# Query order, fill places and mask matmuls in a fused block-sparse, gated LoRA kernel on one Trainium2 core

## The chip, the cores and the metric

The kernel runs on one core of one Trainium2 chip. A core has a matrix engine (TensorE, in the profile PE, with its weight loads as PEld), a vector engine (VectorE, DVE), a scalar engine (ScalarE, ACT), a general engine (GpSimd, POOL) and a queue engine (SyncE, SP). Every engine works through its own list of instructions in order and waits at semaphores for the others. Transfers between the chip's memory and the core's on-chip buffers (DMAs) are issued by SP, ACT and POOL and run beside the engines. Matrix products land in PSUM, a small accumulator memory of which a buffer here holds 128 x 512 values.

The metric is the device time of one execution in microseconds (us). Three runs of the kernel before gave 449.41, 449.87 and 450.09 us; their median, 449.87, is the time before.

## What is computed

The input x is (2, 1024, 1024): two batches of 1024 rows. Cut to what matters:

```python
xn = layernorm(x)                                   # over the last axis, eps 1e-5
bm = (mask summed over each 32 x 32 block) > 0
s  = xn @ (weight * bm spread to blocks).T + bias   # S
q  = xn.mean(over the 1024 rows) @ Wq.T             # one query per batch
c  = softmax(q @ lora_keys.T / sqrt(128))           # 8 coefficients per batch
y  = xn @ W_org.T + sum_e c[e] * (xn @ lora_down[e]) @ lora_up[e]
out = x + s * silu(y)
```

All weights are 1024 x 1024, `lora_down` is 8 x 1024 x 64 and `lora_up` 8 x 64 x 1024.

## The kernel before, in words

**Precision and folding.** A value in float32 is split into a high part that the matrix engine takes (type fp32r) and the remainder; a product is the sum of high x high, high x low and low x high, so that one logical matmul is three on TensorE (lines 453, 456, 457 for S and Y tiles, 417 to 419 for folds, 1216 for the last stage). The low-rank part is not run on x. Instead its weights are folded into W_org, once per batch, since the coefficients differ by batch: a *fold* takes one 128 x 512 piece of W_org transposed and adds the product of `lora_down` with the scaled `lora_up` to it. `y_prep` (L401) loads `ds` and `wo` over the SP queue and splits `ds` into `dhi` (ScalarE, L408) and `dlo` (VectorE, L409); `y_mul` (L412) runs twelve matmuls into a buffer `psw`; `y_sum` (L422, L424) adds `psw` to `wo` on VectorE. `scale_up` (L387) loads four pieces of `lora_up`, scales each by its coefficient on ScalarE (L395) and takes the remainder on VectorE (L396): the four `cut` tiles.

**Stages.** (1) Up to about 90 us a start-up that is ordered by hand: layer-norm statistics of batch 0, its transposes, the first half of S, and the first half of the folded weights for batch 0. (2) `phase("y", 0, 0, ..., jobs_b)`: eight row tiles of Y, 24 matmuls each, and behind each tile one fold of the second half (`mix_jobs`), with statistics of batch 1, the mask of the second half, and the first sums of the transposed batch 1 in `jobs_b`. (3) `phase("y", 0, 1, ..., jobs_c)`: eight more row tiles. Meanwhile `s_mul` (L298) loads a piece of the S weight (`ws`), multiplies it by the block mask `m_sb` (L302) and casts it; `s_lo` (L308, L310) takes the remainder. The query of batch 1 is made here too: `steps[0]` transposes row sums into `xrow` (L325), `steps[1]`, which is `query` (L338), multiplies `xrow` by Wq on VectorE with a running sum (L349) and adds the halves to `qb` (L353). `steps[2]`, `scores` (L358), is set in the middle of row tile 6 by `split_at`: TensorE multiplies `qb` by the keys (L360). (4) Eight row tiles of S (`s_tile`), and between the first five of them the sixteen folds of batch 1, shared out as 4, 4, 3, 3, 2. (5) The last stage computes batch 1 transposed, in eight *units* with seven block products per quadrant in place of eight; the sums of x it needs (`xv`) were stored to memory in stages 2 and 3.

**Fills and unit products.** In stage 4 the sums of x come back: `fill` loads a 128 x 512 piece of `xv` into one of three slots of the buffer `misc` in turn, casts it on ScalarE (L1065) and takes the remainder on VectorE (L1066). The loads of `scale_up(1, 1)`, which the eighth fold issues (`if n == NKT - 1`), use the next three slots of `misc` in the same turn and one buffer of the staging pool. `early` holds the first unit's work on its weights: two mask products (`unit_mask`, L1094) and four block sums (`unit_sum`, L1102). The first five row tiles and their folds are the loop at the end of the change below. `ds`, `wo`, `ws` and `us` share six staging buffers (tag "st"). A `wo` buffer is free when its folded result has been stored to memory (`yu`, issued by ScalarE's queue one fold later, L513).

**The mask.** `mask_part` (L283) loads 128 x 1024 mask values, sums them by rows on ScalarE (L254), and, with the second half of a pair, makes a small tile `r` on VectorE (L264, `mask_spread`), multiplies it by an expansion matrix that lies in `misc[:, 0, :]` (eight matmuls into `mp`, L274, `mask_apply_mm`) and copies the result to `m_sb` (L281, `mask_apply_cp`). `spread_stats` (L927), which follows one of the parts, transposes the statistics of batch 1 into `row_ps` on TensorE (L930).

**Order.** Program order is the order on TensorE, VectorE and ScalarE in stages 2 to 5. The list of the SP queue is arranged when the program is built, so an edit can move a load past others there. In `jobs_b` and `jobs_c` the argument i is the row tile just multiplied; what they yield is emitted behind that tile.

Of the kernel before, what the change touches and what calls it, by code (L numbers as in the profile page):

```python
# [32 lines left out]
def kernel(  # L33
# [102 lines left out]
    def nat_tile(dt=F32):  # L136
        k = turns[0] % 3
        turns[0] += 1
        v = raw_flat[:, k * D : (k + 1) * D]
        return v if dt == F32 else v.bitcast(dt)  # L140
# [107 lines left out]
    def mask_sum(qr, c, mt, eng, part=0):  # L248

        if qr not in msum:  # L250
            msum[qr] = small.tile([P, 2, 2], F32, name="s2")
        o = msum[qr][:, part, c : c + 1]
        if eng is nc.scalar:
            nc.scalar.activation(mt.bitcast(F32), mt, AF.Copy, accum_out=o)  # L254
        else:
            nc.vector.tensor_reduce(o, mt, AX.X, ALU.add)
# [5 lines left out]
    def mask_spread(qr):  # L262
        r4 = small.tile([P, 2, 4], BF16, name="r4")
        nc.vector.scalar_tensor_tensor(  # L264
            r4, msum[qr][:, 0, :].unsqueeze(2).to_broadcast([P, 2, 4]), 0.0,
            pick4.unsqueeze(1).to_broadcast([P, 2, 4]), ALU.is_gt, ALU.mult,
        )
        spread[qr] = r4

    def mask_apply_mm(qr):  # L270
        r4 = spread[qr]
        mp = ps_s.tile([P, NKT, 8], F32, name="mp", tag="ps_s")
        for kt in range(NKT):
            nc.tensor.matmul(  # L274
                mp[:, kt, :], lhsT=expand[:, kt * P : (kt + 1) * P],
                rhs=r4.rearrange("p a b -> p (a b)"), start=True, stop=True,
            )
        spread[qr] = mp

    def mask_apply_cp(qr):  # L280
        nc.vector.tensor_copy(m_sb[:, :, 8 * qr : 8 * (qr + 1)], spread[qr])  # L281

    def mask_part(qr, c, mt=None):  # L283
        if mt is None:
            mt = nat_tile(I32)
        else:
            mt = stage_l.tile([P, D], I32, name="mt", tag="ac", bufs=1)
        nc.sync.dma_start(mt, mask[2 * qr + c])
        mask_sum(qr, c, mt, nc.scalar)
        if c == 1:  # L290
            mask_spread(qr)
            mask_apply_mm(qr)
            mask_apply_cp(qr)

    def new_slot():
        return wpool.tile([P, NKT, 2, NH], F32R, name="slot", tag="w")
# [257 lines left out]
    J = lambda f, *a: (lambda: f(*a))  # L554
# [98 lines left out]
    with tc.manual_schedule(engines={mybir.EngineType.PE, mybir.EngineType.DVE, mybir.EngineType.Activation, mybir.EngineType.Pool}):  # L653
# [237 lines left out]
        def jobs_b(i):  # L891
            if i == 0:
                yield J(scale_up, 0, 1)
            yield J(mix_jobs, y01, 0, 1, i)
            yield J(store_out, 1)
            if i < 3:
                yield J(act_stats, 1 + i)
            for t in ((4,), (5, 6), (7,), (), (), (), (), ())[i]:
                yield J(nat_stats, t)
            yield from {  # L900
                2: [J(mask_part, 2, 0)], 3: [J(mask_part, 2, 1), J(spread_stats), J(mask_part, 3, 0, 1)],
                4: [J(mask_part, 3, 1, 1)],
            }.get(i, ())
            if i == 3:
                yield J(wide_load, 0, 0)
            if i == 4:
                yield J(wide_load, 0, 1)
                yield J(wide_a, 0)
            if i == 5:
                yield J(wide_b, 0)  # L910
                yield J(wide_load, 1, 0)
            if i == 6:
                yield J(wide_a, 1)
            if i == 7:
                yield J(wide_load, 1, 1)
# [63 lines left out]
        def wide_b(j):  # L979
# [12 lines left out]
            store_sums()  # L992

        phase("y", 0, 0, y00, True, jobs_b)


        s1 = new_slot()
        steps = coeffs(1)

        def jobs_c(i):  # L1000
            if i < 2:
                yield J(store_out, 1 - i)

            if i < 6:
                yield J(s_mul, s1, 1, i)
            if i == 5:
                yield steps[0]
                yield steps[1]
            if i == 6:
                yield steps[3]  # L1010
                yield J(scale_up, 1, 0, up_homes)
            if i == 5:
                yield J(s_mul, s1, 1, 6)
                yield J(s_mul, s1, 1, 7)
                for kt in (5, 6, 7):
                    yield J(s_lo, s1, 1, kt)
            if i in (0, 2):
                yield J(wide_load, 2 + i // 2, 0)
                yield J(wide_load, 2 + i // 2, 1)
            if i < 5:  # L1020
                yield J((wide_b, wide_a)[i % 2], 1 + (i + 1) // 2)
                yield J(s_lo, s1, 1, i)

        up_homes = [misc[:, 0, :]]
        split_at[(0, 1, 6)] = steps[2]
        phase("y", 0, 1, y01, False, jobs_c)


        folds = [(h, kt) for h in range(2) for kt in range(NKT)]

        def fold(n):
            h, kt = folds[n]
            if n + 1 < len(folds):
                y_prep(1, *folds[n + 1])
            store_late()
            y_mul(1, h, kt)
            flush()
            y_sum(1, h, kt)
            ps, ws = staged.pop((1, h, kt))
            late_stores.append((  # L1040
                yu[:, :, 2 * h + kt // 4, kt % 4, :].rearrange("u p n -> p u n"),
                ws.rearrange("p (u n) -> p u n", n=P),
            ))
            if n == NKT - 1:
                homes = [misc[:, (len(spare) + k) % 3, :] for k in range(3)]
                spare.extend(homes)
                scale_up(1, 1, homes)
# [23 lines left out]
        def s_tile(i):  # L1071
            store_out()
            flush()
            ps = gemm(0, i, s1)
            pending.append(J(final_evac, "s", 0, 1, i, ps))
# [6 lines left out]
        def unit_load(u, i):  # L1082
            kind, p = units[u]
            src = wu[p] if kind == "s" else yu[p].rearrange("p a j n -> p (a j n)")
            c = slice(2 * i * NH, 2 * (i + 1) * NH)
            nc.sync.dma_start(raw_flat[:, c], src[:, c])
# [45 lines left out]
        def fills(j, n):  # L1132
            for _ in range(n):
                fill(j, ORDER_X[filled[j]])
                filled[j] += 1

        for i, n in enumerate((4, 4, 3, 3, 2)):
            s_tile(i)
            for k in range(n):
                fold(done)  # L1140
                done += 1
                if i < 3 and (i == 2 or k in (1, 2)):
                    fills(0, 1)
                if i > 2 and (i == 4 or k):
                    fills(1, 1)
                if i in (2, 3):
                    early.pop(0)()
            if i == 0:
                unit_load(0, 0)
                unit_load(0, 1)  # L1150
# [219 lines left out]
```

## Time and profile before

| what | value |
|---|---|
| time, median of three runs | 449.87 us (449.41 to 450.09) |
| the profiled execution's own time | 450.43 us |
| its span, first to last instruction | 448.7 us |
| VectorE busy | 288.9 us |
| ScalarE busy | 175.3 us |
| moved to and from memory | 90.58 MB, 202 GB/s over the span |
| TensorE clock granted | full speed in all 40 slices |

The span is what the engines' records cover; the time also holds what lies before and after it. A timeline row reads: start in us, duration, engine, line, operation, output<-inputs, shape, and in brackets the idle time of that engine before the row with what ended it. Matmuls overlap, so a row's duration is longer than the distance to the next start. In the waits view a row names who waited for whom: total us, number of times, longest. SPq and ACTq rows are issues of transfers; a transfer lands some us after its issue (stores of `yu` 2.6 to 7.9 us, median 5.2).

### The profile page before, as it was taken

How to read it: one execution, taken by the hardware profiler on the slowest of the kernel's cores; microseconds unless marked ns; L12 is line 12 of the kernel's file. 1: busy time of each engine (PE TensorE's matmuls, PEld its weight loads, DVE VectorE, ACT ScalarE, POOL GpSimd, SP SyncE). 2: the span in 40 equal slices, each digit the busy share in tenths (PEclk: the TensorE clock that was granted, in tenths of full speed). 3: DMA queues.
4: the chain of work that ended last, by engine and by line, in shares of the span. 5: the costliest groups of instructions: out<-in, count | busy, mean ns of one | idle time of the engine just before them, and what ended most of it. 6: DMA issues, size and time to landing. Idle time of an engine off the chain costs nothing.

```text
span 448.7 us, 5791 instructions
## 1 busy us (share of the span) xinstructions
PE 437.7 (98%) x2058; PEld 363.1 (81%) x2058; DVE 288.9 (64%) x478; ACT 175.3 (39%) x291; POOL 76.5 (17%) x93
## 2 busy tenths in 40 slices
PE   7999999999999999989999999999999999999996
PEld 5789888888878888878888788887888888888885
DVE  5989777756627768855456586578466295455625
ACT  3676626454631222224233234176354422441520
POOL 3784310002320313120000000110020020002000
PEclk9999999999999999999999999999999999999999
DMA  8995406687896799895979898966174247219103
GB/s 266 390 351 203 151 25 200 220 256 192 281 294 196 249 265 314 284 368 166 242 226 314 236 289 260 259 166 210 48 159 145 72 106 177 93 16 220 47 1 117
DMA packets 47741, 90.58 MB, mean 202 GB/s; under 512 B 4816, under 2 KB 15328, under 8 KB 47712
## 3 DMA queue, kind: packets, MB, share of 16 engines
q1 hardware_dynamic: 30624, 66.08, 44.6%
q0 software_dynamic: 6624, 16.26, 15.7%
q10 hardware_dynamic: 10464, 7.87, 5.3%
q8 instruction: 16, 0.26, 0.2%
q14 instruction: 13, 0.11, 0.1%
HBM read 70.26 MB, written 19.93 MB: 201 GB/s over the span
## 4 chain that ended last, share of the span: by engine, by line
PE 68%; DVE 12%; DMA 10%; issue 6%; ACT 3%; POOL 1%; SPq 0%; ACTq 0%; DVEq 0%; POOLq 0%
PE acc_ps L1216 24%; PE py L1216 10%; PE acc_ps L457 7%; PE acc_ps L453 7%; PE acc_ps L456 7%; PE psw L419 4%; PE psw L417 4%; PE psw L418 4%; DMA ws<-in_wT_dram 3%; DMA stash<-in_x_dram 2%; DVE st L148 1%; DMA raw<-in_x_dram 1%; DVE slot L594 1%; DMA misc<-in_up_dram 1%; DMA raw<-in_mask_dram 1%
## 5 line engine op out<-in xcount | busy, mean ns | idle before, releaser
L1216 PE MATMUL acc_ps<-xw,ow 128*128 128x512 f32 (+1 forms) x492 | 112.0, 384 | 0.0
L453 PE MATMUL acc_ps<-slot,xgrp 128*128 128x512 f32 (+1 forms) x288 | 106.5, 370 | 0.1
L457 PE MATMUL acc_ps<-slot,xgrp 128*128 128x512 f32 (+1 forms) x288 | 105.6, 367 | 0.7 <-DVE xgrp L606 0.7
L456 PE MATMUL acc_ps<-slot,xgrp 128*128 128x512 f32 (+1 forms) x288 | 105.7, 367 | 0.6 <-DVE slot L594 0.4
L1216 PEld LDWEIGHTS acc_ps<-xw,ow 128*128 128x128 f32 x492 | 90.8, 188 | 18.7 <-ACT acc_ps L1276 0.5
L456 PEld LDWEIGHTS acc_ps<-slot,xgrp 128*128 128x128 f32 x288 | 54.3, 189 | 10.6 <-DVE slot L594 2.1
L457 PEld LDWEIGHTS acc_ps<-slot,xgrp 128*128 128x128 f32 x288 | 54.2, 188 | 10.3 <-DVE xgrp L606 1.1
L453 PEld LDWEIGHTS acc_ps<-slot,xgrp 128*128 128x128 f32 x288 | 54.3, 188 | 9.1 <-DVE stash L469 0.3
L419 PE MATMUL psw<-cut,dlo 128*128 128x512 f32 x128 | 49.9, 390 | 0.8 <-DVE dlo L409 0.8
L418 PE MATMUL psw<-cut,dhi 128*128 128x512 f32 x128 | 49.8, 389 | 0.0
L417 PE MATMUL psw<-cut,dhi 128*128 128x512 f32 x128 | 49.8, 389 | 0.0
L1216 PE MATMUL py<-xw,ow 128*128 128x512 f32 x192 | 46.3, 389 | 0.0
L1216 PEld LDWEIGHTS py<-xw,ow 128*128 128x128 f32 x192 | 36.0, 188 | 7.5
L1109 DVE TENSOR_TENSOR ow<-raw,ow 128x1024 fp32r<-128x1024 f32 (+1 forms) x32 | 34.5, 1087 | 10.2 <-ACT ow L1108 10.2
L408 ACT CAST dhi<-ds 128x512 fp32r<-128x512 f32 x32 | 19.7, 616 | 45.6 <-DMA ds<-in_down_dram 32.5
L505 POOL DMA_DIRECT2D stash<-in_x_dram x16 | 14.4, 899 | 120.7 <-DVE stash L502 120.7
L409 DVE TENSOR_TENSOR dlo<-ds,dhi 128x512 fp32r<-128x512 f32 x32 | 22.0, 688 | 14.8 <-ACT dhi L408 14.8
L424 DVE TENSOR_TENSOR wo<-wo,psw 128x512 f32<-128x512 f32 x32 | 21.9, 685 | 13.0 <-PE psw L419 12.8
L1108 ACT CAST ow<-raw 128x1024 fp32r<-128x1024 f32 (+1 forms) x32 | 29.4, 939 | 2.1 <-DVE wo L424 1.6
L419 PEld LDWEIGHTS psw<-cut,dlo 128*128 128x128 f32 x128 | 24.0, 188 | 6.2 <-DVE dlo L409 1.3
L418 PEld LDWEIGHTS psw<-cut,dhi 128*128 128x128 f32 x128 | 24.0, 188 | 5.0
L417 PEld LDWEIGHTS psw<-cut,dhi 128*128 128x128 f32 x128 | 24.0, 188 | 4.9
(180 smaller groups left out, 468.4 us busy)
## 6 DMA issues: line engine op xcount, KB each, us to landing
ds<-in_down_dram SPq DMA_DIRECT2D x32, 256.0 KB, 3.8
wo<-in_worgT_dram SPq DMA_DIRECT2D x32, 256.0 KB, 4.2
raw<-in_x_dram SPq DMA_DIRECT2D x11, 512.0 KB, 4.8
stash<-in_x_dram POOLq DMA_DIRECT2D x16, 256.0 KB, 5.2
raw<-in_wu_dram SPq DMA_DIRECT2D x8, 512.0 KB, 5.2
yu<-wo ACTq DMA_DIRECT2D x16, 256.0 KB, 5.2
raw<-yu SPq DMA_DIRECT2D x8, 512.0 KB, 3.8
out_dram<-stash ACTq DMA_DIRECT2D x14, 256.0 KB, 3.9
```

What stands on the lines that cost most here:

```text
L408: nc.scalar.copy(dhi, ds)
L409: nc.vector.tensor_tensor(dlo, ds, dhi.bitcast(F32), ALU.subtract)
L417: nc.tensor.matmul(ps, lhsT=dhi[:, c, :], rhs=u[c][:, 0, :], start=c == 0, stop=False)
L418: nc.tensor.matmul(ps, lhsT=dhi[:, c, :], rhs=u[c][:, 1, :], start=False, stop=False)
L419: nc.tensor.matmul(ps, lhsT=dlo[:, c, :], rhs=u[c][:, 0, :], start=False, stop=c == 3)
L424: nc.vector.tensor_tensor(ws, ws, ps, ALU.add)
L453: nc.tensor.matmul(ps, lhsT=xs[:, kt, 0, cols], rhs=w[:, kt, 0, wc], start=kt == 0, stop=False)
L456: nc.tensor.matmul(ps, lhsT=xs[:, kt, 0, cols], rhs=w[:, kt, 1, wc], start=False, stop=False)
L457: nc.tensor.matmul(ps, lhsT=xs[:, kt, 1, cols], rhs=w[:, kt, 0, wc], start=False, stop=kt == NKT - 1)
L1108: nc.scalar.copy(o[:, a:b, 0], raw[:, a:b])
L1109: nc.vector.tensor_tensor(o[:, a:b, 1], raw[:, a:b], o[:, a:b, 0].bitcast(F32), ALU.subtract)
L1216: nc.tensor.matmul(ps, lhsT=o[:, a, wl, j, :], rhs=xw[j][:, m, xl, cols], start=start and j == 0 and k == 0, stop=j == 3 and k == 2, skip_ ...
```

## The change

Three edits. The mask's matmuls and copy (`mask_apply`) are taken out of `mask_part` and called one row tile later, behind that tile's fold; the small tile `r` is still made at once. In row tile 5 of stage 3 the query (`steps[0]` and `steps[1]`) is emitted ahead of the sixth `s_mul`, not behind it. In stage 4 the seven fills of the first x tile go behind folds 1, 2, 3, 4, 5, 9 and 10, where they went behind folds 1, 2, 5, 6, 8, 9 and 10 (counted from 0), and the six early products of the first unit behind folds 8, 11, 12, 13, 14 and 15, where they went behind folds 8 to 13.

```diff
@@ mask_part @@
         if c == 1:
             mask_spread(qr)
-            mask_apply_mm(qr)
-            mask_apply_cp(qr)
+
+    def mask_apply(qr):
+        mask_apply_mm(qr)
+        mask_apply_cp(qr)
@@ jobs_b @@
                 2: [J(mask_part, 2, 0)], 3: [J(mask_part, 2, 1), J(spread_stats), J(mask_part, 3, 0, 1)],
-                4: [J(mask_part, 3, 1, 1)],
+                4: [J(mask_apply, 2), J(mask_part, 3, 1, 1)], 5: [J(mask_apply, 3)],
@@ jobs_c @@
-            if i < 6:
-                yield J(s_mul, s1, 1, i)
             if i == 5:
                 yield steps[0]
                 yield steps[1]
+            if i < 6:
+                yield J(s_mul, s1, 1, i)
             if i == 6:
                 yield steps[3]
                 yield J(scale_up, 1, 0, up_homes)
@@ row tiles and folds of stage 4 @@
             for k in range(n):
                 fold(done)
                 done += 1
-                if i < 3 and (i == 2 or k in (1, 2)):
+                if i < 3 and k in ((1, 2, 3), (0, 1), (1, 2))[i]:
                     fills(0, 1)
                 if i > 2 and (i == 4 or k):
                     fills(1, 1)
-                if i in (2, 3):
+                if (i, k) in ((2, 0), (3, 0), (3, 1), (3, 2), (4, 0), (4, 1)):
                     early.pop(0)()
```

## The prediction

> **What bounds the kernel now.** I read the busy table, then TensorE's own waits, then its timeline from 50 us to the end, and last the timelines of VectorE, ScalarE and the SP queue around each wait.
>
> ```profile
> span 448.7 us, 5791 instructions
> PE 437.7 (98%) x2058; PEld 363.1 (81%) x2058; DVE 288.9 (64%) x478; ACT 175.3 (39%) x291; POOL 76.5 (17%) x93
> ...
> PE sp L360 <- DVE qb L353: 1.4, 1, 1.4
> PE mp L274 <- DVE r L264: 1.2, 2, 0.6
> PE psw L419 <- DVE dlo L409: 0.8, 1, 0.8
> ...
> 62.34 0.40 PE L457 MATMUL acc_ps<-slot,xgrp 128*128 128x512 f32 x1
> 63.03 0.40 PE L456 MATMUL acc_ps<-slot,xgrp 128*128 128x512 f32 x1
> ...
> 123.14 0.39 PE L419 MATMUL psw<-cut,dlo 128*128 128x512 f32 x1
> 124.12 0.34 PE L274 MATMUL mp<-r,misc 128*128 128x8 bf16 x8 [0.59 <-DVE r L264]
> 124.65 0.39 PE L456 MATMUL acc_ps<-slot,xgrp 128*128 128x512 f32 x1
> ...
> 132.40 0.39 PE L419 MATMUL psw<-cut,dlo 128*128 128x512 f32 x1
> 133.17 0.39 PE L456 MATMUL acc_ps<-slot,xgrp 128*128 128x512 f32 x1
> ...
> 193.50 0.39 PE L457 MATMUL acc_ps<-slot,xgrp 128*128 128x512 f32 x1
> 195.31 0.36 PE L360 MATMUL sp<-keys_sb,qb 128*128 128x8 f32 x2 [1.43 <-DVE qb L353]
> 195.84 0.40 PE L456 MATMUL acc_ps<-slot,xgrp 128*128 128x512 f32 x1
> ...
> 247.56 0.39 PE L418 MATMUL psw<-cut,dhi 128*128 128x512 f32 x1
> 248.78 0.50 PE L419 MATMUL psw<-cut,dlo 128*128 128x512 f32 x1 [0.83 <-DVE dlo L409]
> 249.12 0.40 PE L417 MATMUL psw<-cut,dhi 128*128 128x512 f32 x1
> ```
>
> TensorE starts a 128x512 matmul every 0.227 us (the 24 of the tile at 220.12 end at 225.56). From 50 us on this pitch breaks in three places only, the three waits shown (the other 0.6 us of the mp row is at 12 us). So TensorE sets the end, an engine off it counts only where TensorE waits for it, and a wait's price is read from starts, not from the idle column: start to start less the same stretch without the wait.
>
> **The change, part by part.** *Mask matmuls a tile later.* Between 123.14 and 124.65 lie 1.51 us. The second mask's eight matmuls between the same neighbours take 133.17 - 132.40 = 0.77 us. The row_ps transpose in the first stretch I take at 0.11 us (eight L325 transposes fit between 189.88 and 191.21: 1.33 less two pitches, by 8). So the wait costs 1.51 - 0.77 - 0.11 = 0.63 us. It arises because the mask sum waits for its load (ScalarE's sum ends at 123.87) and VectorE's r follows at 123.90. Moved behind the next tile's product, the matmuls find r some 8 us old; the second set moves to about 140.3, and its r (132.4) is as old. What stood behind them, row_ps, waits for the statistics, whose last power starts on GpSimd at 119.65: no wait. What is moved with them: the PSUM copies to m_sb (0.14 us more on VectorE before the work at 142.75, with dlo due only at 146.6), and in the built order the SP queue's load of misc (133.02, it overwrites the expansion weights) goes behind the ws load at 142.29. Its reader is at 201.39; m_sb's first reader is at 162.36. Both covers are over 20 us. Gain 0.63, from the idle column 0.59.
>
> *Query ahead of the sixth S weight.* The VectorE rows:
>
> ```profile
> 189.56 0.68 DVE L310 TENSOR_TENSOR slot<-ws,slot 128x512 fp32r<-128x512 f32 x1
> 192.92 0.69 DVE L302 TENSOR_TENSOR ws<-ws,m_sb 128x512 f32<-128x512 f32 x1 [2.68 <-DMA ws<-in_wT_dram]
> 193.53 0.68 DVE L349 SCALAR_TENSOR_TENSOR junk<-xrow,misc 128x512 f32<-128x512 f32 x1
> 194.87 0.29 DVE L353 TENSOR_TENSOR qb<-qh 128x128 f32<-128x128 f32 x1
> ```
>
> VectorE is idle for 2.68 us before the s_mul at 192.92, which waits for its load, while the query behind it has had its rows since 191.1 (190.10 + 1.03). Ahead of it the query starts when the s_lo ends (190.24), and qb is there after 194.87 + 0.29 - 193.53 = 1.63 us, at 191.9 (with 0.3 to spare for the second row). TensorE, 0.63 us early, asks at 193.73 - 0.63 = 193.1: no wait, 1.2 us of spare. The s_mul still starts when its load lands, so it loses nothing; the softmax comes some 1.5 us earlier, as VectorE does the three s_mul and three s_lo without a break. The price of the wait: 195.84 - 193.50 = 2.34, against 63.03 - 62.34 = 0.69 for the same two matmuls unhindered: 1.65 us (idle column 1.43).
>
> *Fills and unit products over the folds.* Call T the start of the ninth fold (241.88), index 8. The eleventh's L419 is due at T + 5.44 + 0.45 = T + 5.89 and ran at T + 6.90; between its neighbours 249.12 - 247.56 = 1.56 less two pitches leaves 1.11 us lost. Its dlo started at 248.04 = T + 6.16, and TensorE followed 0.74 later. VectorE was held by the third scaled up-tile, then ran without a break:
>
> ```profile
> 236.35 0.46 SPq L392 DMA_DIRECT2D misc<-in_up_dram  x1
> ...
> 241.69 0.72 ACT L395 ACTIVATE cut<-misc,c 128x512 fp32r<-128x512 f32 x1 [2.00 <-DMA misc<-in_up_dram]
> ```
>
> Two things change. (a) The fill behind fold 8 goes, one xw subtraction of 0.60 us (start to start). (b) Fills now lie at folds 1, 2, 3, 4, 5; the last misc slot that an up-tile takes is free one fold (2.72 us) sooner. That load now stands behind the wo load of 234.49 (which waits for the store issued at 229.19, 5.3 us) and goes out at about T - 7.0 where it went at T - 5.5. So dlo of fold 9 starts near T + 0.5 (it was T + 1.90), the evacuation pair follows (0.72, 0.61), and the sum of fold 8 is then held by its own matmuls, at T + 2.72 + 0.19 = T + 2.91 (fold 7 ends at 236.44, its sum starts at 236.63). Then 0.60, the unit's mask product 1.14, dlo at T + 4.65, TensorE at T + 5.39: due at 5.89, no wait, 0.5 spare. With (a) alone: 6.16 - 0.60 + 0.74 = 6.30, 0.41 us of wait stay. So the third part gives 0.70 to 1.11; I take 1.11, since the slot's release is certain in the built order.
>
> What is late next: the subtractions added before dlo of folds 6 and 7 leave these 1.1 us spare (fold 6: sum, fill and dlo end 0.19 + 0.60 + 0.60 + 0.68 = 2.07 after fold 4's end, due 3.17 after it). The mask product moved to fold 11 delays fold 13's dlo: its sum starts at T + 16.51, mask 17.11, dlo 18.25, TensorE 18.99, due 19.49; if dlo of fold 12 comes as late as now (258.06, T + 15.08 without the wait), the chain of 3.22 + 0.54 + 0.74 ends at 19.58: 0.09 lost. The last sum (0.60) now stands before the ow splits (278.15); these are needed at 292.16.
>
> The Trainium skill, in VectorE: DVE Perf Modes, The DRAIN you can't avoid, says that the next operation waits until the pipe is empty. The rows start 0.60 us apart with 0.69 us durations, so the pages' main rule is not what they show; by it sum, mask and dlo would come some 0.17 us later, 0.3 us of the spare 0.5 would stay, and the sum would not change.
>
> Sum: 0.63 + 1.65 + 1.11 = 3.39 us (2.85 by idle columns, the other bound). The profiled execution took 450.43 with a span of 448.7, 1.7 around it, and lies 0.56 above the runs' median of 449.87. Its span becomes 445.3, it 447.0, and the median 449.87 - 3.39 = 446.5. The tail from 292 us is unchanged TensorE work at its pitch.
>
> **The rivals.** *The third wait stays in part.* It needs the up-load to land no sooner, for instance when the store before the wo load takes its longest 7.9 us rather than 5.3: 0.41 to 1.11 us less, 446.9 to 447.6, say 447.2. For it: transfers are 98% busy from 238 to 252 us, at 316 GB/s. Against: slices there reach 404 to 410.
>
> *The transfers set the folds.* TensorE arrives 2.28 us earlier, the loads and stores don't, and folds 10 to 13 give all back: 449.9. For it: fold 13's dlo was ready only 0.27 us before its use (261.52 + 0.74 against 262.53). Against: each yu store is issued when a fold's sum is done, so the chain moves with TensorE; from 205 to 222 us transfers are busy 72% at 192 GB/s.
>
> *Slower: the staging buffers' rotation.* In the built order wo of fold 10 no longer waits for the fourth scaled tile but for the landing of fold 7's store, and ds of fold 11 and every SP load behind it wait too. That store goes out with the fourth scaling, near T - 0.8, and lands 4.5 to 7.9 later, so ds goes out at T + 4 to T + 7.5 (now T + 2.6). With its median landing of 4.4, 0.62 for dhi and 0.74, it is in time until T + 8.3 (due at T + 14.05); later, each us costs one. It decides, and undoes all gains and 0.9 more, from a store landing of some 13 us: 451. The longest shown is 7.9.
>
> **How the numbers follow.** Forecast 446.5: 65%, its own range 446.0 to 447.2 (the idle-column bound is 447.0; the runs spread by 0.35 to each side). Third wait in part, 447.2: 22%. Transfers set the folds, 449.9: 7%. Slower, 451: 6%. Over 0.2% (0.9 us, about what a measurement of this kernel can tell from no change) faster: 65 + 22 = 87%; within: 7%; slower: 6%. The range goes from 446.0 to 448.3, which leaves the two last cases out.
>
> **What would show it.** Right: sp, psw and the later mp are gone from TensorE's waits and the starts keep 0.227 us; qb ends near 192, ahead of the s_mul; dlo of fold 10 starts 1.2 us or more before its matmul is due. Wrong: a new psw wait on dlo or cut at folds 8 to 13, a wait of sp that stays, or a third misc up-load that lands after T - 1.

## The result, and the profile after

| comparison (each on its own chip) | after, median (range, runs) | before, median (runs) | ratio, 95% interval |
|---|---|---|---|
| first | 448.71 us (447.67 to 452.76, 22) | 449.45 us (22) | 0.9989 (0.9973 to 1.0006) |
| second, `after_again` | 448.27 us (447.04 to 449.64, 12) | 449.93 us (23) | 0.9970 (0.9954 to 0.9987) |
| third, `after_third` | 448.87 us (447.90 to 451.80, 12) | 449.82 us (29) | 0.9979 (0.9955 to 1.0002) |

The ratios are formed from the fast runs alone (456.43 us, one slow run of before in the third comparison, is not in its ratio) and are not the quotients of the medians. Taken alone, the first and the third comparison do not tell the change from none. Weighted by the inverse of their variances the three give 0.9979 (0.9969 to 0.9990): the change saves 0.9 us (0.5 to 1.4). Forecast were 3.39 us, and a time of 446.5 us (446.0 to 448.3). The direction is right; about a quarter of the size came.

The head of the page and the waits view of after, TensorE's part (who waits <- for whom: total us, times, longest):

```profile
span 446.9 us, 5791 instructions
PE 438.8 (98%) x2058; PEld 363.3 (81%) x2058; DVE 289.1 (65%) x478; ACT 175.4 (39%) x291; POOL 76.4 (17%) x93
...
PE warm L677 <- DVE ones_r L96: 1.1, 1, 1.1
PE acc_ps L1218 <- ACT acc_ps L1278: 0.8, 1, 0.8
...
PE mp L274 <- DVE r L264: 0.3, 1, 0.3
PE psw L419 <- ACT dhi L410: 0.3, 1, 0.3
```

sp is gone, psw on dlo is gone, and what is left of mp is the one at 12 us. In their place stand two that the view of before did not have: the first quadrant product (L1218) waits for a copy on ScalarE (L1278), and a fold for `dhi` (L410). From L295 on, lines of after are two higher than before's.

TensorE's timeline of after at the three old places and the two new ones (start, duration, engine, line, operation, and in brackets idle time and what ended it):

```profile
122.89 0.39 PE L421 MATMUL psw<-cut,dlo 128*128 128x512 f32 x1
123.12 0.27 PE L932 MATMUL row_ps<-ident,mr 128*16 128x128 f32 x1
123.15 0.48 PE L455 MATMUL acc_ps<-slot,xgrp 128*128 128x512 f32 x1
...
192.91 0.28 PE L362 MATMUL sp<-keys_sb,qb 128*128 128x8 f32 x2
193.04 0.48 PE L455 MATMUL acc_ps<-slot,xgrp 128*128 128x512 f32 x1
...
245.09 0.39 PE L420 MATMUL psw<-cut,dhi 128*128 128x512 f32 x1
245.31 0.39 PE L421 MATMUL psw<-cut,dlo 128*128 128x512 f32 x1
...
258.23 0.39 PE L421 MATMUL psw<-cut,dlo 128*128 128x512 f32 x1
258.88 0.51 PE L419 MATMUL psw<-cut,dhi 128*128 128x512 f32 x1 [0.26 <-ACT dhi L410]
259.23 0.39 PE L420 MATMUL psw<-cut,dhi 128*128 128x512 f32 x1
259.61 0.50 PE L421 MATMUL psw<-cut,dlo 128*128 128x512 f32 x1
...
302.97 2.88 PE L1218 MATMUL py<-xw,ow 128*128 128x512 f32 x12
306.66 5.76 PE L1218 MATMUL acc_ps<-xw,ow 128*128 128x512 f32 x24 [0.81 <-ACT acc_ps L1278]
```

The first three groups run at the pitch. The fourth does not: 259.61 - 258.23 is 1.38 where three pitches are 0.68, and the start after it adds 0.11: 0.81 us lost at the fourteenth fold (fold 13). The fifth: 306.66 - 302.97 = 3.69 where twelve matmuls are 2.72: 0.97 lost. In before the same place lost 0.20 and 0.12 us, too little for a bracket with idle time:

```profile
305.60 2.88 PE L1216 MATMUL py<-xw,ow 128*128 128x512 f32 x12
308.52 5.73 PE L1216 MATMUL acc_ps<-xw,ow 128*128 128x512 f32 x24
314.09 2.88 PE L1216 MATMUL py<-xw,ow 128*128 128x512 f32 x12
```

Where the new waits come from, in the ScalarE, SP and GpSimd timelines of after (ACTq and SPq rows, and GpSimd's DMA rows, are issues):

```profile
243.06 0.37 ACTq L515 DMA_DIRECT2D yu<-wo  x1
...
258.21 0.62 ACT L410 CAST dhi<-ds 128x512 fp32r<-128x512 f32 x1 [6.65 <-DMA ds<-in_down_dram]
...
289.94 0.36 ACTq L522 DMA_DIRECT2D out_dram<-stash  x1
290.39 1.14 ACT L1067 CAST xw<-xs 128x512 fp32r<-128x512 f32 x2 [11.57 <-DMA stash<-in_x_dram]
...
305.08 1.05 ACT L1110 CAST ow<-raw 128x1024 fp32r<-128x1024 f32 x1 [0.43 <-DMA out_dram<-stash]
306.03 0.58 ACT L1278 COPY acc_ps<-acc_ps 128x512 f32<-128x512 f32 x1
```

```profile
250.69 0.33 SPq L407 DMA_DIRECT2D wo<-in_worgT_dram  x1
251.12 0.39 SPq L1066 DMA_DIRECT2D misc<-xv  x1
251.60 0.46 SPq L405 DMA_DIRECT2D ds<-in_down_dram  x1
```

```profile
297.14 0.87 POOL L507 DMA_DIRECT2D stash<-in_x_dram  x1 [10.36 <-DVE stash L504]
...
302.68 0.58 POOL L522 DMA_DIRECT2D out_dram<-stash  x1 [4.09 <-DMA stash<-in_x_dram]
```

Fold 8's result goes out at 243.06; the `wo` load that takes its buffer can be issued only when that store has landed, at 250.69, 7.6 us later. In SP's queue the `ds` load of fold 13 stands behind it, goes out at 251.60 and lands 6.6 us later, and `dhi` starts at 258.21: TensorE had wanted it at 258.46. The second wait: ScalarE's queue holds a store of `stash` that needs the landing of an accumulate (a transfer that adds x to `stash`) issued by GpSimd at 282.64. That landing took 7.3 us, and the four fills of the quadrant, behind the store, started at 290.39, 1.1 us after TensorE had begun the quadrant (289.25). In before, where the quadrant began at 292.00, the store was out earlier and the fills started 0.2 us behind it:

```profile
290.91 0.36 ACTq L520 DMA_DIRECT2D out_dram<-stash  x1
292.20 2.18 ACT L1065 CAST xw<-xs 128x512 fp32r<-128x512 f32 x4 [10.63 <-PE acc_ps L457]
```

Behind the fills VectorE finishes the last tile, and GpSimd issues the last accumulate (297.14 in after) and, when that has landed, its store (302.68). Later in ScalarE's queue the cast of `ow` waits for the landing of that store, and the copy that TensorE needs stands behind the cast.

### The profile page after: what moved, and what is told of

Read it like the earlier page. It is cut to its first block, busy times and chain, and to the rows that moved or that the text cites. A ratio compares the mean times of both kernels' runs of the same rounds, so it can differ in the third digit from the quotient of the medians.

```text
span 446.9 us, 5791 instructions
## 1 busy us (share of the span) xinstructions
PE 438.8 (98%) x2058; PEld 363.3 (81%) x2058; DVE 289.1 (65%) x478; ACT 175.4 (39%) x291; POOL 76.4 (17%) x93
## 4 chain that ended last, share of the span: by engine, by line
PE 53%; issue 33%; POOL 5%; DVE 4%; DMA 3%; ACT 0%; SPq 0%; POOLq 0%; ACTq 0%; DVEq 0%
PE acc_ps L1218 22%; PE py L1218 9%; PE acc_ps L459 5%; PE acc_ps L455 5%; PE acc_ps L458 5%; PE psw L421 2%; PE psw L419 2%; PE psw L420 2%; POOL xv L529 2%; POOL stash L507 2%; DMA raw<-in_x_dram 1%; DVE slot L596 1%; DMA stash<-in_x_dram 1%; DVE ramp L587 1%; DVE st L148 1%
## 5 line engine op out<-in xcount | busy, mean ns | idle before, releaser
L1218 PE MATMUL acc_ps<-xw,ow 128*128 128x512 f32 (+1 forms) x492 | 112.2, 384 | 0.8 <-ACT acc_ps L1278 0.8
L1218 PEld LDWEIGHTS acc_ps<-xw,ow 128*128 128x128 f32 x492 | 90.7, 188 | 19.7 <-ACT acc_ps L1278 1.2
L1218 PE MATMUL py<-xw,ow 128*128 128x512 f32 x192 | 46.3, 389 | 0.0
L1218 PEld LDWEIGHTS py<-xw,ow 128*128 128x128 f32 x192 | 36.0, 188 | 7.5
L410 ACT CAST dhi<-ds 128x512 fp32r<-128x512 f32 x32 | 19.7, 617 | 46.7 <-DMA ds<-in_down_dram 28.6
```

The source lines that it names most:

```text
L1218: nc.tensor.matmul(ps, lhsT=o[:, a, wl, j, :], rhs=xw[j][:, m, xl, cols], start=start and j == 0 and k == 0, stop=j == 3 and k == 2, skip_ ...
```

## The experiments

Measured beside the times is the time that TensorE lost at each place: for successive rows from 52 us on, the distance of their starts less 0.227 us for each matmul of the earlier row, counted where it is over 0.095 us. It includes the slow restart behind a wait. "mp" is both masks, "162" the products with the last of the eight weight pieces in the first row tile of stage 3, which starts at 156 us, "f7", "f9", "f10", "f13" the folds counted from 0, "quad" the first quadrants of the last stage. One row is one profiled execution; bold marks a wait that the edit takes away.

| kernel | mp | 162 | sp | f7, f9 | f10 | f13 | quad | sum | span |
|---|---|---|---|---|---|---|---|---|---|
| before, first profile | 0.75 | 0 | 1.58 | 0 | 1.11 | 0 | 0.33 | 3.77 | 448.7 |
| `b0_again` | 0.36 | 0.45 | 0.61 | 0 | 0.51 | 0 | 0.39 | 2.31 | 447.1 |
| `before_third` | 1.17 | 0.36 | 1.06 | 0 | 0.30 | 0 | 0.46 | 3.35 | 448.1 |
| `units_only` | 1.08 | 0 | 1.69 | 0 | 0.62 | 0 | 0.60 | 3.99 | 448.6 |
| `query_only` | 0.10 | 0 | **0** | 0 | 0.33 | 0 | 0.80 | 1.22 | 445.4 |
| `mask_only` | **0** | 0 | 0.18 | 0 | 1.18 | 0 | 0.13 | 1.49 | 446.3 |
| `mask_query` | **0** | 0.43 | **0** | 0 | 1.21 | 0 | 0.13 | 1.76 | 446.4 |
| `mask_query_again` | **0** | 0.61 | **0** | 0 | 0.45 | 0 | 0.57 | 1.62 | 446.3 |
| `mask_query_store` | **0** | 0 | **0** | 0.52 | 1.21 | 0 | 0.98 | 2.70 | 447.6 |
| `mask_query_early_fill` | **0** | 1.10 | **0** | 0 | 0.23 | 0 | 0.66 | 1.98 | 446.9 |
| `folds_only` | 0.17 | 0 | 0.72 | 0 | **0** | 0 | 1.21 | 2.11 | 446.7 |
| `fills_only` | 0.31 | 0 | 0.55 | 0.99 | **0** | 0 | 1.95 | 3.82 | 448.7 |
| after, first profile | **0** | 0 | **0** | 0 | **0** | 0.81 | 1.13 | 1.94 | 446.9 |
| `after_again` | **0** | 1.34 | **0** | 0 | **0** | 0.56 | 0.46 | 2.36 | 447.0 |
| `after_third` | **0** | 0.84 | **0** | 0 | **0** | 0.38 | 0.73 | 1.94 | 446.8 |
| `after_store_moved` | **0** | 1.24 | **0** | 0 | **0** | 0 | 1.22 | 2.45 | 446.7 |
| `last_fold_swapped` | **0** | 0 | **0** | 0.54 | **0** | 0.24 | 0.83 | 1.60 | 446.2 |

For the three profiles of before, span less sum is 444.9, 444.8 and 444.8, for the three of after 445.0, 444.6 and 444.9. The places of the table hold nearly all that differs between them.

Three theories stood at the start. A: the three waits are worth some 3.4 us in every execution, and the folds part brings two new ones. B: the waits hang on landings and differ from execution to execution, and the first profile showed them long. C: whatever TensorE gains early it gives back later, since the transfers come no sooner.

**The kernel before, twice more.** No edit.

> The kernel before, a second time. Theory A (the three waits are worth about 3.4 us in every execution, and the folds edit brings two new waits, fold 13's L419 at about 0.8 us and quad 0's copy L1276 at about 0.9 us): the idle columns of sp, mp and psw L419 read 1.4, 0.6 and 0.8 again, each to 0.2; quad 0's wait for the copy costs 0.2 as before. Theory B (the waits hang on landings and vary, the profiled execution of before was a long one): their sum is 0.8 us or more below the first profile's 2.85. Ratio 1.000 either way.

> The kernel before, a third time. If the first profile showed its waits near their largest: mp, sp and psw of fold 10 cost 1.5 to 2.3 us together (3.4 in the first, 1.5 in the second). If the second was the exception: 3 us or more. Quad 0's copy 0.1 to 0.4.

The second took 449.12 us median, ratio 1.0004 (0.9980 to 1.0029); the third execution 449.77. TensorE's part of the waits view, `b0_again` first, then `before_third`:

```profile
PE sp L360 <- DVE qb L353: 0.4, 1, 0.4
PE mp L274 <- DVE r L264: 0.4, 2, 0.2
...
PE psw L419 <- DVE dlo L409: 0.2, 1, 0.2
```

```profile
PE mp L274 <- DVE r L264: 1.4, 3, 0.6
...
PE sp L360 <- DVE qb L353: 0.9, 1, 0.9
```

Same program, and sp waits 0.4, 0.9 or 1.4 us. The three waits cost 3.44 us in the first profile, 1.48 in the second, 2.53 in the third. The third lies a little over the 2.3 us that B allowed, and far under the first. So B is right for these waits: the first profile was a long one. For sp, what differs is the `ws` load that held VectorE in front of the query: VectorE starts 6.6 us behind its issue in the first, 5.9 and 6.2 in the others.

**One part at a time.** `query_only` and `mask_only` are the second and the first edit of the change alone, `folds_only` the third:

```diff
@@ query_only @@
-            if i < 6:
-                yield J(s_mul, s1, 1, i)
             if i == 5:
                 yield steps[0]
                 yield steps[1]
+            if i < 6:
+                yield J(s_mul, s1, 1, i)
@@ mask_only @@
-            mask_apply_mm(qr)
-            mask_apply_cp(qr)
...
-                4: [J(mask_part, 3, 1, 1)],
+                4: [J(mask_apply, 2), J(mask_part, 3, 1, 1)], 5: [J(mask_apply, 3)],
@@ folds_only @@
-                if i < 3 and (i == 2 or k in (1, 2)):
+                if i < 3 and k in ((1, 2, 3), (0, 1), (1, 2))[i]:
...
-                if i in (2, 3):
+                if (i, k) in ((2, 0), (3, 0), (3, 1), (3, 2), (4, 0), (4, 1)):
```

> The query moved alone. Theory A: sp's wait is gone, no new wait at fold 13 or quad 0 beyond 0.3 us: 1.65 us less than before, ratio 0.9963. Theory B: the ratio is nearer 0.998, since the wait is shorter in most executions. Theory C (TensorE that arrives earlier, by whichever part, meets transfers that come no sooner): quad 0's wait for its copy grows by 0.5 us or more, and the ratio is 0.998 or above.

> The mask matmuls a tile later alone. Theory A: mp's later wait is gone, nothing new: 0.63 us less than before, ratio 0.9986. Theory B: 0.9986 or nearer 1, the wait of mp hangs on a load. Theory C: quad 0's wait grows by 0.2 to 0.5 us and the ratio is 0.9995 or above.

> Fills, unit products and early spread over the folds in the other way, alone. Theory A: psw of fold 10 no longer waits, but fold 13 waits for dhi (0.5 to 0.8 us) and quad 0 waits for its copy (0.8 to 1 us), as with all three parts: -1.11 + 0.8 + 0.8 = 0.5 us more than before, ratio 1.001. Theory B: wait of fold 10 gone, 0.998. Theory C: one of the two new waits is missing (TensorE arrives 2.3 us later than with all three parts): ratio 0.998 to 0.999.

Measured: query 448.27 us, ratio 0.9983 (0.9959 to 1.0007); mask 448.69, 0.9991 (0.9967 to 1.0016); folds 449.61, 1.0021 (0.9994 to 1.0048). Each takes away its wait. For query and mask the ratios lie nearer B's numbers than A's, though no interval excludes either. The folds part alone is not a gain: fold 10 no longer waits, but the quadrant loses 1.21 us. Here TensorE comes later than in after, so C does not explain that place; A's wait at fold 13 did not come. That one of the two new waits is missing is what C had said, but not the ratio, 0.998 to 0.999. For C speaks also the quadrant of `query_only`, 0.80 with the fills as before. ScalarE's timeline of `folds_only` at the quadrant:

```profile
289.83 0.36 ACTq L520 DMA_DIRECT2D out_dram<-stash  x1
290.29 1.15 ACT L1065 CAST xw<-xs 128x512 fp32r<-128x512 f32 x2 [11.83 <-DMA stash<-in_x_dram]
```

The same picture as in after: the accumulate, issued at 282.26, takes 7.6 us, and the fills wait for it.

**Which half of the folds part.** `units_only` moves only the unit's products, `fills_only` only the fills:

```diff
@@ units_only @@
-                if i in (2, 3):
+                if (i, k) in ((2, 0), (3, 0), (3, 1), (3, 2), (4, 0), (4, 1)):
@@ fills_only @@
-                if i < 3 and (i == 2 or k in (1, 2)):
+                if i < 3 and k in ((1, 2, 3), (0, 1), (1, 2))[i]:
```

> The first unit's products moved to later folds, alone; the fills stay. Nothing ahead of the ninth fold changes and the built order keeps the staging buffers of the kernel before, so fold 10's wait for dlo stays (0.3 to 1.2 us), the xs loads take 2 to 4 us, quad 0's copy costs 0.1 to 0.4. That the wait of fold 10 goes with this part would be against the second step's reading (the fill and the up-load).

> The fills spread over the folds in the other way, the unit's products and the mask parts as before. In the built order this alone turns the rotation of the staging buffers, so that the third xs load waits for the last fold's store. If the rotation makes quad 0 late: the four xs loads take about 10 us on the SP queue (3.5 before), the first fills wait for the stash accumulate and quad 0's copy costs 0.5 us or more. psw of fold 10: 0 to 0.4.

One execution each: 450.3 and 450.4 us. With the units alone fold 10 still loses 0.62 us; with the fills alone it loses nothing. So the gain at fold 10 is the fills', as the prediction read it. So are the losses: with the fills alone fold 7 waits for `dhi` (0.99) and the quadrants lose 1.95; with the units alone the quadrant loses 0.60, somewhat over before's 0.33 to 0.46 and the 0.4 expected.

**Without the folds part.** Mask and query together, the last hunk of the change left out, once beside other kernels and once beside after:

```diff
-                if i < 3 and k in ((1, 2, 3), (0, 1), (1, 2))[i]:
+                if i < 3 and (i == 2 or k in (1, 2)):
...
-                if (i, k) in ((2, 0), (3, 0), (3, 1), (3, 2), (4, 0), (4, 1)):
+                if i in (2, 3):
```

> Mask and query parts without the folds part. The five profiles so far give the means of three waits where they are not edited away (excess of starts over the pitch): mp 0.32 us, sp 0.77, psw of fold 10 0.77. Theory B (the profile of before showed all three near their largest, the typical gain is their mean): mp and sp gone, 1.1 us less, ratio 0.9976; psw of fold 10 stays between 0.3 and 1.2; quad 0's copy 0.1 to 0.7. Theory A (the waits of the first profile, 2.3 us for the two): ratio 0.995. Theory C (whatever TensorE gains ahead of quad 0 is lost at quad 0 to transfers that come no sooner): quad 0 loses 1 us or more, ratio 0.999 or above.

> Mask and query parts without the folds part, a second time, beside the changed kernel on the same chip. If the folds part gives back at folds 7 and 13 and at quad 0 more than it takes at fold 10 (over the profiles so far: 0.5 and 0.9 us more against 0.8 less): no dhi wait at folds 7 to 13, quad 0 at 0.1 to 0.6, psw of fold 10 at 0.3 to 1.2; 0.3 to 1 us faster than the changed kernel of this call, ratio to before 0.996 to 0.998. If the folds part is worth its 0.8 us: 0.5 us or more slower than the changed kernel.

> The changed kernel, a third time, beside the kernel without its folds part. Over its two profiles so far it lost 2.1 and 2.4 us behind 50 us: the third loses 1.5 to 2.5, of it 0.3 to 1.3 at quad 0 and 0 to 0.8 at folds 7 and 13; sp, the later mp and psw of fold 10 don't wait. Ratio 0.997 to 0.999.

448.35 us, 0.9988 (0.9971 to 1.0005), and 448.67, 0.9975 (0.9951 to 1.0000), beside after's 448.87, 0.9979 (0.9955 to 1.0002), on the same chip. No fold waits for `dhi`, and the quadrant loses 0.13 and 0.57: C, which asked for 1 us or more there, falls. The first gains less than the 0.9976 of theory B; in its profile fold 10 took 1.21 us, the longest of all, and 162 us 0.43. ScalarE's row of the first fills in `mask_query`:

```profile
289.42 0.36 ACTq L522 DMA_DIRECT2D out_dram<-stash  x1
289.96 1.14 ACT L1067 CAST xw<-xs 128x512 fp32r<-128x512 f32 x2 [10.62 <-PE acc_ps L459]
```

Here the store does not hold the fills; they wait for TensorE's last tile. Whether after or the kernel without its folds part is the better one, the times don't tell: their medians lie 0.2 us apart, where 0.3 to 1 was expected.

**Moving the store that holds the fills.** In after, and in the kernel without the folds part, the store in front of the quadrant's fills is left to GpSimd:

```diff
         def s_tile(i):
-            store_out()
+            if i < 7:
+                store_out()
```

> The changed kernel, with one output store of tile 5 issued by GpSimd ahead of its next stores instead of by ScalarE ahead of quad 0's fills. If ScalarE's queue, held by that store until the accumulate of stash has landed, makes quad 0's copy late, the fills start within 0.3 us of quad 0's start (1.14 before), the copy's wait of 0.97 falls to 0.2 or less, and the ratio is 0.9966 (0.9989 less 1.0 us). If instead the fills wait for the xs loads or for TensorE's sums, the wait stays at 0.7 or more and the ratio at 0.999. Fold 13's wait for dhi: 0 to 0.8, by the landings.

> Mask and query parts, without the folds part, and with that store issued by GpSimd. Only psw of fold 10 is left (0.3 to 1.2): 1.4 us less than before by the means of the waits, ratio 0.997. Theory C: a wait elsewhere behind 205 us takes 0.5 us or more of it, ratio 0.998 or above.

Half of it came. GpSimd's and ScalarE's timelines of `after_store_moved`:

```profile
295.97 0.87 POOL L507 DMA_DIRECT2D stash<-in_x_dram  x1 [9.42 <-DVE stash L504]
296.59 1.38 POOL L522 DMA_DIRECT2D out_dram<-stash  x2
302.24 0.54 POOL L522 DMA_DIRECT2D out_dram<-stash  x1 [4.27 <-DMA stash<-in_x_dram]
```

```profile
289.22 2.18 ACT L1067 CAST xw<-xs 128x512 fp32r<-128x512 f32 x4 [10.62 <-PE acc_ps L459]
...
304.85 1.05 ACT L1111 CAST ow<-raw 128x1024 fp32r<-128x1024 f32 x1 [0.42 <-DMA out_dram<-stash]
305.80 0.58 ACT L1279 COPY acc_ps<-acc_ps 128x512 f32<-128x512 f32 x1
```

The fills start when TensorE is done, and the next accumulate goes out 1.17 us sooner than in after (295.97 against 297.14), of which 0.23 is that this quadrant begins sooner (289.02 against 289.25). But the store behind it goes out 6.3 us after that, where it was 5.5 in after (302.68 - 297.14), with a second store of 256 KB issued between them; the quadrant still loses 1.22 us. So the held fills are shown to delay the chain by the other 0.94 us, and in this profile moving their store does not take the wait away: it comes back as a longer landing, 5.7 us for the last accumulate where the other sixteen profiles have 4.7 to 5.2. Time: 447.97 us, 0.9983 (0.9968 to 0.9999), not told apart from after. In the kernel that had no held fills the same move looks like a loss: quadrant 0.98 instead of 0.13 and 0.57, 449.42 us, 1.0005 (0.9991 to 1.0019), where 0.997 was expected and `mask_query` beside it had 448.35. The number is the one put down for theory C, but `mask_query`, where TensorE comes as early, does not have this loss. The 0.52 us in the table at f9 are a wait for a `cut` tile, in this profile alone.

**Is it the rotation of the staging buffers?** In the built order of after the third `xs` load waits for the store of the last fold, in before for that fold's `dlo`. Swapping the last fold's two requests gives before's wait back:

```diff
     def y_prep(b, h, kt):
+        last = (b, h, kt) == (1, 1, NKT - 1)
+        if last:
+            ws = stage.tile([P, NH], F32, name="wo", tag="st", bufs=6)
+            nc.sync.dma_start(ws, worgT[kt * P : (kt + 1) * P, h * NH : (h + 1) * NH])
         ds = stage.tile([P, 4, P], F32, name="ds", tag="st", bufs=6)
         nc.sync.dma_start(ds, down[kt])
-        ws = ...
+        if not last:
+            ws = ...
```

> The changed kernel, with the last fold's two loads asked for in the other order, so that each takes the other's staging buffer; then the third xs load waits for the last fold's dlo and not for its store, as in the kernel before. If the rotation makes quad 0 late: the four xs loads take 2 to 4 us instead of 10, the accumulate lands within 6.9 us, the fills start within 0.3 us of the quad, the copy's wait falls from about 1.2 to 0.4 or less: ratio 0.9965 to 0.9975. If TensorE's earlier arrival alone makes it late: the wait stays at 0.8 or more and the ratio at 0.999.

> The changed kernel, a second time. If quad 0's wait belongs to the change: the four xs loads take about 10 us on the SP queue again, the first accumulate of stash lands 7.3 us or more after its issue (5.5 to 6.9 in the five profiles with the staging buffers as before), the copy's wait costs 0.8 to 1.3 us again. If it is chance: 0.1 to 0.4 as in the kernel before. Fold 13's wait for dhi: 0 or 0.8, by the landings. Ratio 0.9985 to 0.9995.

Not settled, and rather against it. Swapped, the `xs` loads take 5.2 us instead of 9.8 and the accumulate lands in 6.8, but the quadrant still loses 0.83 (448.35 us, 0.9974, 0.9954 to 0.9994). And after, a second time, keeps the 9.8 us while its accumulate lands in 6.4 and the quadrant loses 0.46 (448.27 us, 0.9970). The four slow `xs` loads alone do not decide.

That second profile shows a third place. ScalarE and TensorE in `after_again`:

```profile
160.87 0.34 ACTq L522 DMA_DIRECT2D out_dram<-stash  x1
161.25 0.62 ACT L429 CAST slot<-wo 128x512 fp32r<-128x512 f32 x1 [5.26 <-DMA stash<-in_x_dram]
```

```profile
161.92 0.50 PE L455 MATMUL acc_ps<-slot,xgrp 128*128 128x512 f32 x1 [0.58 <-ACT slot L429]
162.65 0.50 PE L458 MATMUL acc_ps<-slot,xgrp 128*128 128x512 f32 x1 [0.22 <-DVE slot L437]
```

Again a store on ScalarE's queue waits for an accumulate (issued at 150.98, landed 9.9 us later), and a cast that TensorE needs stands behind it: 1.34 us. Over the nine profiles with both mask and query moved the place loses 0.62 us in the mean, over the other eight 0.10. `mask_only` has 0 there, and the query comes later than 162 us, so it can only be the mask edit's or chance.

**Only the fill.** Mask and query, and of the folds part one fill: the one behind the ninth fold goes behind the fourth.

```diff
-                if i < 3 and (i == 2 or k in (1, 2)):
+                if i < 3 and k in ((1, 2, 3), (1, 2), (1, 2))[i]:
```

> Mask and query parts, the unit's products as before, and of the folds part only the fill: the one behind the ninth fold goes behind the fourth. In the built order the staging buffers keep the rotation of the kernel before for the third xs load. The prediction's part (a): fold 10's wait falls by 0.6 to 0.7 us, to 0.1 to 0.6. If the rotation brings the new waits: no dhi wait at folds 7 to 13, quad 0 at 0.1 to 0.6, and 0.5 us faster than the mask and query parts alone, ratio 0.995 to 0.997. If any move of a fill brings them: quad 0 at 0.8 or more, or a dhi wait of 0.5, and no gain over them.

Fold 10 loses 0.23, with no wait for `dhi` at any fold, and the quadrant 0.66: the fold's part comes as expected, the gain over mask and query alone does not show in the time (448.58 us, 0.9977, 0.9956 to 0.9997); in the profiled execution 1.10 us went at 162 us. Its lowest run, 446.87 us, is the lowest of this comparison, but it is not told apart from after.

**The two open places, over all 17 traces.** *At 162 us* the loss follows one difference. The accumulate that holds ScalarE's store lands 8.9 to 10.0 us after its issue, and it is issued 5.0 to 7.6 us ahead of the row tile that needs the cast. Where the first less the second is at most 3.1 us nothing is lost; from there on each us costs one: 3.45 gives 0.36 (`before_third`), 3.94 gives 0.84 (`after_third`), 4.44 gives 1.34 (`after_again`), and no profile is off by more than 0.1. So the held store is the cause there in every profile. The lead is 6.1 us in the mean of the ten profiles with the mask edit and 6.6 in the other seven, at the same mean landing (9.6 and 9.5): TensorE comes sooner and the accumulate does not, as theory C has it. The groups overlap (5.0 to 7.6 and 6.3 to 7.1), so that share of the mask edit is likely, not shown.

*At the quadrant* two lengths add up to the loss, within 0.1 us: by how much the fills start later than 0.2 us behind the start of the quadrant, and by how much GpSimd's last store goes out later than 5.3 us behind the last accumulate (the two profiles with the moved store left out). The six profiles with the new fills start them 0.93 us behind in the mean, the nine without 0.24; the second length is the same, 5.6 and 5.7 us. So what the new fills cost there is the held store; in `query_only` too it held the fills, by 0.35 us. The accumulate that holds it is issued 6.6 to 6.8 us ahead of the quadrant in every profile, so it comes as much sooner as TensorE does, against C. It lands after 6.4 to 8.1 us with the new fills and after 5.5 to 6.9 without; what lengthens it is open.

## Why the prediction was wrong, by its steps

**What held.** Every wait named went, each by the part named for it, and the arithmetic of the third is confirmed to a few hundredths. From T = 239.42 in after, dlo of fold 10 was put at T + 4.65 = 244.07 and its matmul at T + 5.89 = 245.31. VectorE's rows, the matmul being the 245.31 row above:

```profile
191.26 0.29 DVE L355 TENSOR_TENSOR qb<-qh 128x128 f32<-128x128 f32 x1
191.47 0.69 DVE L304 TENSOR_TENSOR ws<-ws,m_sb 128x512 f32<-128x512 f32 x1
...
242.94 1.22 DVE L1096 TENSOR_TENSOR raw<-raw,m_sb 128x1024 f32<-128x1024 f32 x1
244.08 0.69 DVE L411 TENSOR_TENSOR dlo<-ds,dhi 128x512 fp32r<-128x512 f32 x1
```

`qb` is done at 191.55, in front of the s_mul, and 1.4 us before sp. `row_ps` follows without a wait. The slower rival's store landing of 13 us did not come: the longest one between the folds that a wait shows is fold 8's, 7.6 to 7.8 us in all three profiles of after.

**The step that failed first: "Sum: 0.63 + 1.65 + 1.11 = 3.39 us".** These are the waits of one execution, and the prediction took them off the median of all runs, though it noted that this execution lay 0.56 us above it. Over three profiles of before they cost 0.76, 1.08 and 0.64, together 2.48; over all profiles that still have the wait 0.56 (seven), 0.91 (seven, from 0.18 to 1.69) and 0.77 (nine). So 0.9 us of the sum was that execution's alone. For the same reason the range was too narrow: "the runs spread by 0.35 to each side" came from three runs; 22 runs of before went from 448.01 to 451.53.

**The second: what is late next.** "From 50 us on this pitch breaks in three places only" and "The tail from 292 us is unchanged TensorE work at its pitch" were not so: the first profile already lost 0.33 us at the quadrant, in distances too small for the bracket with idle time. And fold 13 was given 0.09 us at worst. The mean over three profiles each rises at fold 13 from 0 to 0.58, at the quadrant from 0.39 to 0.77 and at 162 us from 0.27 to 0.73: 1.42 us come back. 2.48 - 1.42 = 1.06, against 0.9 (0.5 to 1.4) in the times; with three profiles each this is an estimate.

At folds 7 and 13 the return belongs to the fills: seven profiles with the new spread lose 0.50 us there in the mean, ten without it nothing. The pattern stood in the slower rival: `wo` of fold 10 waits for fold 7's store, and `ds` of fold 11 behind it. It was followed for that pair alone, with the median landing of `ds`, 4.4 us. One turn later it is fold 8's store, `wo` of fold 12 and `ds` of fold 13, and there, in the three profiles of after, the store took 7.6 to 7.8 us and the load 6.0 to 6.6. Whether TensorE's earlier arrival has a part in it is open: `folds_only` and `fills_only`, where it comes later, lose nothing at fold 13. At the quadrant, profiles with the new fills lose 1.05 in the mean and those without 0.45, not counting the two with the moved store; the difference is the held store, clear in four of the six (`folds_only`, `fills_only`, after, `last_fold_swapped`), though single profiles of the two groups overlap (0.46 against 0.80). At 162 us it is the held store again, which the prediction did not look at.

The rival "the transfers set the folds" named the right place, fold 13 with the 0.27 us that `dlo` had to spare, and was wrong that folds 10 to 13 give all back. Its reason, that the transfers come no sooner, is not what after shows there: fold 8's store goes out 3.64 us behind the start of that fold in all three profiles, so it moves with TensorE, and what came late were two long landings.

## What to carry to other kernels

A wait that ends with a landing is a sample, not a price: profile the same kernel two or three times before taking its idle columns off a median, and price a saving by the mean. Then list, for the engine that sets the end, the places whose input is ready only shortly before its use (0.27 us at fold 13), small excesses without a bracket too; when the engine comes earlier or a queue is rearranged, each of them can take some of the gain. A store that ScalarE issues and that needs another transfer's landing held every cast behind it here, at 161 us and at 290 us.

## What the runs showed of the hardware that was not expected

Landings differ by place and by execution while the work is the same. Accumulates of 256 KB landed after 4.7 to 5.7 us at 297 us, 5.5 to 8.1 at 283 us, and 8.9 to 10.0 at 151 us. The Trainium skill, in DMA: Bandwidth & Descriptors, Anatomy of one DMA — SWDGE (gpsimd) path, fits one DMA as 2.0 us and its bytes at 436 GB/s, from which I estimate 2.6 us for 256 KB. These runs, with other transfers under way, are above it by a factor of about two to four; an accumulate that is alone was not run.

A short wait costs TensorE more than its idle column, by about 0.3 us (0.26 to 0.32) at each fold and quadrant of these profiles that shows a bracket. At fold 10 of before the bracket says 0.83 us and the starts lose 1.10, 0.99 at the wait and 0.11 at the next start; in `b0_again` it is 0.24 and 0.50. At fold 13 of after the bracket says 0.26 us, and the starts lose 0.42 at the wait and 0.12 at the next. The 0.15 and 0.11 that follow there are a second wait, without a bracket: the matmul at 259.61 starts 0.75 us after its `dlo` (258.86), as the one of fold 10 in before started 0.74 after its own.
